# Rank terms on four row tiles of the array, from copies loaded four times over, in a low-rank modulated linear kernel

## The chip, the cores and the metric

The kernel runs on one core of a Trainium2 chip. The metric is device time in microseconds (us) for one launch, the median of three runs. The profile shows one execution; its engines are PE (the matrix engine, with its weight loads on the row PEld), DVE, ACT, POOL and SP.

## The reference, cut to what matters

Eight batches `b` of 1024 rows `t` and 512 features are sent through two layers with a residual sum each. The first layer's matrix belongs to the batch: a shared base plus a term of rank 8, whose factors come out of a small network on the condition vector. The second layer scales a shared weight by the condition on both sides.

```python
ae = layernorm(cond); h = gelu(ae @ w1 + b1); xw = h @ w2 + b2
x_a, x_b = split(xw)                        # each (b, 512, 8)
layer = base + einsum('bdr,bkr->bdk', x_a, x_b)
x = x + (x + einsum('btc,bco->bto', x, layer))
ys = cond / sqrt(512); d = rsqrt(einsum('bi,io->bo', ys*ys, weight*weight) + 1e-8)
x = x + einsum('bsi,io->bso', x * ys[:, None], weight) * d[:, None]
```

## The kernel before

The two layers and both residual sums are folded into one 512 x 512 matrix per batch, P(b) = (2I + base + A(b) B(b)^T) N(b), where N(b) = I + diag(ys) weight diag(d). P(b) is built in the tile `q[b]` as (2I + base) N(b) plus the rank term A(b) T(b), with T(b) = B(b)^T N(b), a product of small inner dimension. Then out = x P(b).

Matrices are held as a rounded part and a rest (`ph`, `pl` of `q`; the two halves of `xs` for x; `nh`, `nl` of N), and a product is three matmuls: high by high, high by low, low by high.

**The factors.** `stack` makes, for each group g of four batches, a tile `sa[g]` with A and a tile `stt[g]` with T. Their 128 partitions are four blocks of 32, one per batch: in a block lie the 8 ranks with their splits into high and low parts, so that one matmul over the 32 rows gives the rank term to full precision. Since the four batches share a tile, `mask_t` (line 487) multiplies `stt[g]` by a 0/1 column and so keeps one batch's 32 rows; `rank_term` (line 492) then contracts over all 128 rows, for one block `c` of 128 output rows.

**Setup** (lines 81 to 786) runs in an order written out by hand: weight loads, the small network (`px` gathers h @ w2; its matmuls run on column tiles of 32), the factors, the bases of batches 0 to 3 in units of six matmuls (`Fill`), and batch 0 whole. Here the buffers of PSUM are `misc` (2), `px` (2) and `acc` (4).

**Main stage** (lines 788 to 862). `main(b, t)` is 12 matmuls into one of four `po` buffers, a copy on ACT and a store. It runs 64 times; place i = 8b + t is the slot after the i-th of them. Everything else of batches 1 to 7 is put behind a place with `at(...)`:

- Batches 1 to 3: `rank_p` (line 634), one column block behind each of the places first+1 to first+4 with first = 0, 8, 16. It takes a `po` buffer, runs one matmul and adds the result to `q[b]` on DVE. `split_p` follows, which rounds half of `q[b]` into `ph` on ACT and subtracts into `pl` on DVE.
- Batches 4 and 5, and 6 and 7, are built in pairs by seven products in two halves each (`Pair`, 14 units of six matmuls, first = 14 and 29), which use the four `acc` buffers. Half of the rank terms are matmuls added into a product's own buffer (products 3 and 4, lines 598 and 599); the other half come from `ranks_11` and `ranks_22` at first+12 and first+13, in `po` buffers.

PE instructions are pinned in program order. In the main stage a scheduler orders DVE, ACT, POOL and SP instructions ahead of time; each engine then runs its queue strictly in order and waits on semaphores. A buffer of a pool is given out again when its last reader is done: `acc` has four, used in turn.

Of the kernel before, what the change touches and what calls it, by code (L numbers as in the profile page):

```python
# [7 lines left out]
F32 = mybir.dt.float32  # L8
F32R = mybir.dt.float32r
# [5 lines left out]
P = 128  # L15
NB = 8
NT = 1024
D = 512
KC = D // P
# [11 lines left out]
def cond_resid_kernel(ctx: ExitStack, tc: tile.TileContext, small, cond, condrows, consts,  # L31
# [10 lines left out]
    nc = tc.nc  # L42

    def mm(*args, **kw):
        tc.keep_in_program_order(nc.tensor.matmul(*args, **kw))  # L45
# [18 lines left out]
    ve, se, sy = InOrder(nc.vector), InOrder(nc.scalar), InOrder(nc.sync)  # L64

    cp = ctx.enter_context(tc.tile_pool(name="cp", bufs=1))
    npool = ctx.enter_context(tc.tile_pool(name="npool", bufs=2))
    ppool = ctx.enter_context(tc.tile_pool(name="ppool", bufs=2))
    big = ctx.enter_context(tc.tile_pool(name="big", bufs=9))
    dram = ctx.enter_context(tc.tile_pool(name="dram", bufs=1, space=bass.MemoryType.DRAM))  # L70
    acc = ctx.enter_context(tc.tile_pool(name="acc", bufs=4, space=PSUM))
    setup = ctx.enter_context(ExitStack())
    misc = setup.enter_context(tc.tile_pool(name="misc", bufs=2, space=PSUM))
    xps = setup.enter_context(tc.tile_pool(name="xps", bufs=1, space=PSUM))
    sp = setup.enter_context(tc.tile_pool(name="sp", bufs=1))

    def big_tile(name, dtype=F32):
        return big.tile([P, KC, D], dtype, tag="big", name=name)
# [20 lines left out]
    mask = cst[:, 2 * P + 5 + NB:2 * P + 5 + NB + 4]  # L99
# [61 lines left out]
    def newton_rsqrt(v, sd, shape, name):  # L161

        r = sp.tile(shape, F32, name=f"r_{name}")
        ve.reciprocal(r, sd)
        t = sp.tile(shape, F32, name=f"t_{name}")
        ve.tensor_mul(t, r, r)
        ve.tensor_mul(t, t, v)
        ve.tensor_scalar(t, t, -0.5, 1.5, ALU.mult, ALU.add)
        return r, t
# [12 lines left out]
    r, t = newton_rsqrt(ve_l, sd, [NB, 1], "l")  # L182
# [30 lines left out]
    q = {0: big_tile("q_0")}  # L213
# [71 lines left out]
    r, t = newton_rsqrt(v, sv, [P, KC, NB], "d")  # L285
# [19 lines left out]
    def work_tile():  # L305
        turns[0] += 1
        return work[:, turns[0] % KC, :]
# [99 lines left out]
    def split(src):  # L407
# [3 lines left out]
        ve.scalar_tensor_tensor(s, hi.bitcast(F32), neg_u, src, ALU.mult, ALU.add)  # L411
        return s

    def stack(srcs, neg, name, g):

        ps = misc.tile([P, D], F32, tag="misc", name=f"ps_{name}{g}")
        for i, src in enumerate(srcs):
            mm(ps, sel[:, g, :], src, start=(i == 0), stop=(i == len(srcs) - 1))
        hi = work_tile()
        se.copy(hi, ps)  # L420

        def rest():
            s = cp.tile([P, D], F32R, name=f"st_{name}{g}")
            ve.scalar_tensor_tensor(s, hi.bitcast(F32), neg, ps, ALU.mult, ALU.add)
            return s

        return rest
# [47 lines left out]
    def add_base(b):  # L475
        for c in range(KC):
            ve.tensor_add(q[b][:, c, :], q[b][:, c, :], b_nat[0][:, c, :])
# [6 lines left out]

    tm = {}

    def mask_t(b):
        g, i = divmod(b, 4)
        tm[b] = npool.tile([P, D], F32R, tag="tm", name=f"tm_{b}", bufs=2)
        ve.tensor_scalar_mul(tm[b], stt[g].bitcast(F32), mask[:, i:i + 1])  # L490

    def rank_term(ps, b, c, first):
        mm(ps, sa[b // 4][:, c * P:(c + 1) * P], tm[b], start=first, stop=True,
           skip_group_check=not first)

    class Base:

# [19 lines left out]
                self.at += 1  # L517

    class Pair:

# [60 lines left out]
        def unit(self):  # L584
            p, s = self.todo.pop(0)
            b, w, z = self.b, ("w", s), ("z", s)
            key = w if p in (1, 6, 7, 4) else z
            first = p in (1, 5, 2)
            if first:
                self.bank[key] = acc.tile([P, D], F32, tag="acc", name=f"pp_{b}_{p}_{s}")  # L590
            if (p, s) in ((1, 0), (6, 0)):
                i = b + (p == 6)
                q[i] = big_tile(f"q_{i}")
            bank = self.bank[key]
            self.product(p, s, bank, first)
            c11, c21 = q[b][:, s, :], q[b][:, 2 + s, :]
            c12, c22 = (q[b + 1][:, s, :], q[b + 1][:, 2 + s, :]) if b + 1 in q else (None, None)
            if p in (3, 4):
                rank_term(bank, b + (p == 3), s + 2 * (p == 4), False)
            if p == 1:  # L600
                se.copy(c11, bank)
            elif p == 5:
                se.copy(c21, bank)
            elif p == 6:
                se.copy(c12, bank)
            elif p == 3:
                ve.tensor_add(c12, bank, c12)
            elif p == 7:
                se.copy(c22, bank)
                ve.tensor_add(c22, c22, c21)  # L610
            elif p == 2:
                ve.tensor_add(c11, bank, c11)
            else:
                se.copy(c21, bank)
# [7 lines left out]
    def p_tiles(b):  # L622
        ph[b] = ppool.tile([P, KC, D], F32R, tag="ph", name=f"ph_{b}")
        pl[b] = ppool.tile([P, KC, D], F32R, tag="pl", name=f"pl_{b}")

    def split_p(b, j, part=None):

        at = slice(2 * j, 2 * j + 2)
        if part != 1:
            se.copy(ph[b][:, at, :], q[b][:, at, :])  # L630
        if part != 0:
            ve.tensor_sub(pl[b][:, at, :], q[b][:, at, :], ph[b][:, at, :].bitcast(F32))

    def rank_p(pool, tag, b, c):

        ps = pool.tile([P, D], F32, tag=tag, name=f"pr_{b}_{c}")
        rank_term(ps, b, c, True)
        ve.tensor_add(q[b][:, c, :], ps, q[b][:, c, :])

    xs = {}  # L640

# [2 lines left out]
    def load_x(b, h):  # L644
        raw[b, h] = big_tile(f"x_{b}_{h}")
        sy.dma_start(raw[b, h], x[b, h])

    def split_x(b, j, part=None):

        t = raw[b, j // 2][:, :, (j % 2) * 2 * P:(j % 2 + 1) * 2 * P]  # L650
        if part != 1:
            xs[b, j] = big.tile([P, 2, KC, 2 * P], F32R, tag="big", name=f"xs_{b}_{j}")
            se.copy(xs[b, j][:, 0], t)
        if part != 0:
            ve.tensor_sub(xs[b, j][:, 1], t, xs[b, j][:, 0].bitcast(F32))


    stt, sa = [None, None], [None, None]
# [86 lines left out]
    next(steps)  # L745
    w2_group()
    next(steps)
    mask_t(0)
    add_base(0)
    fill.units(2)  # L750
    fill.make_n(3, 0)
# [13 lines left out]
    fill.units(3)  # L765
    fill.make_n(3, 1)
    p_tiles(0)
    rank_p(misc, "misc", 0, 0)
    rank_p(misc, "misc", 0, 1)
    fill.round(3, 1)  # L770
    fill.units(2)
    split_p(0, 0, 0)
    rank_p(misc, "misc", 0, 2)
    rank_p(misc, "misc", 0, 3)
    split_p(0, 0, 1)
    fill.finish(3, 1)
    split_p(0, 1)
# [11 lines left out]
    po = ctx.enter_context(tc.tile_pool(name="po", bufs=4, space=PSUM))  # L789
# [18 lines left out]
    def at(b, t, f, *args):  # L808
        after.setdefault((b, t), []).append((f, args))
# [1 line left out]
    def new_pair(b):  # L811
        pairs[b] = Pair(b)

    def ranks_22(b):
        for i in range(2):
            rank_p(po, "po", b + 1, 2 + i)

    def ranks_11(b):
        for i in range(2):
            rank_p(po, "po", b, i)  # L820

    pairs = {}
    place = lambda i: divmod(i, NTT)
    for b in range(1, 4):
        first = (b - 1) * NTT
        for c in range(KC):
            at(*place(first + 1 + c), rank_p, po, "po", b, c)
            if c % 2:
                at(*place(first + 1 + c), split_p, b, c // 2)
    for b, first in ((4, 14), (6, 29)):  # L830

        at(*place(first - 9), load_d, b)
        at(*place(first - 6), new_pair, b)
        for n, p in enumerate(Pair.ORDER):
            at(*place(first - 5 + 2 * n), lambda b=b, p=p: pairs[b].early(p))
            at(*place(first - 2 + 2 * n), lambda b=b, p=p: pairs[b].prepare(p))
            for i in range(2):
                at(*place(first + 2 * n + i), lambda b=b: pairs[b].unit())
        at(*place(first + 5), mask_t, b + 1)
        at(*place(first + 7), mask_t, b)  # L840
        at(*place(first + 12), ranks_11, b)
        at(*place(first + 13), ranks_22, b)
        at(*place(first + 13), split_p, b, 0)
        at(*place(first + 14), split_p, b, 1)
        at(*place(first + 19), split_p, b + 1, 0)
        at(*place(first + 21), split_p, b + 1, 1)

    for b in range(NB):
        for t in range(NTT):
            last = b == NB - 1 and t == NTT - 1  # L850
            if t == 0 and b + 1 < NB:
                p_tiles(b + 1)
                if b < 3:
                    mask_t(b + 1)
            main(b, t, ((0, D // 2), (D // 2, D)) if last else ((0, D),))
            i = b * NTT + t
            if t % 4 == 0 and i + 4 < NB * NTT:
                load_x(*divmod(i // 4 + 1, NHALF))
            if t % 2 == 0 and i + 4 < NB * NTT:
                split_x(*divmod(i // 2 + 2, NTT // 2))  # L860
            for f, args in after.get((b, t), ()):
                f(*args)
# [69 lines left out]
```

## Time and profile before

| | |
|---|---|
| median of three runs | 305.82 us (305.3 to 306.11) |
| the profiled execution | 305.47 us, of which span 303.7 us |
| PE busy | 298.0 us, 98% |
| PEld busy | 227.9 us, 75% |
| DVE busy | 176.4 us, 58% |
| ACT busy | 145.9 us, 48% |
| POOL busy | 5.2 us, 2% |
| granted PE clock, mean | 0.998 |

1.8 us of the profiled execution lie around its span. Busy time of PE counts a matmul to its end, and matmuls overlap one another: of those with 512 columns each lasts about 0.39 us and the next starts 0.23 us after it. What a matmul costs a full queue is thus the distance of starts, which the timeline view gives, and not its duration.

### The profile page before, as it was taken

How to read it: one execution, taken by the hardware profiler on the slowest of the kernel's cores; microseconds unless marked ns; L12 is line 12 of the kernel's file. 1: busy time of each engine (PE TensorE's matmuls, PEld its weight loads, DVE VectorE, ACT ScalarE, POOL GpSimd, SP SyncE). 2: the span in 40 equal slices, each digit the busy share in tenths (PEclk: the TensorE clock that was granted, in tenths of full speed). 3: DMA queues.
4: the chain of work that ended last, by engine and by line, in shares of the span. 5: the costliest groups of instructions: out<-in, count | busy, mean ns of one | idle time of the engine just before them, and what ended most of it. 6: DMA issues, size and time to landing. Idle time of an engine off the chain costs nothing.

```text
span 303.7 us, 3551 instructions
## 1 busy us (share of the span) xinstructions
PE 298.0 (98%) x1369; PEld 227.9 (75%) x1369; DVE 176.4 (58%) x262; ACT 145.9 (48%) x212; POOL 5.2 (2%) x14
## 2 busy tenths in 40 slices
PE   8999999999999999999999999999999999999995
PEld 3655565466888888888888888888888888888884
DVE  4779830979678479977456478981266543600000
ACT  4756132256476564355664454743645546621221
POOL 0011000001000000100000000000000000000000
PEclk9999999999999999999999999999999999999999
DMA  6999999642319636631651134354151545322222
GB/s 204 409 427 419 410 421 419 220 188 69 138 69 343 242 124 226 228 120 69 207 193 52 69 108 171 97 162 192 69 207 69 190 178 212 148 106 104 96 76 105
DMA packets 15952, 57.37 MB, mean 189 GB/s; under 512 B 1840, under 2 KB 2352, under 8 KB 11584
## 3 DMA queue, kind: packets, MB, share of 16 engines
q1 hardware_dynamic: 6064, 38.78, 34.5%
q10 hardware_dynamic: 9360, 16.78, 14.7%
q0 software_dynamic: 512, 1.59, 1.6%
q8 instruction: 10, 0.16, 0.2%
q14 instruction: 6, 0.05, 0.1%
HBM read 40.35 MB, written 16.79 MB: 188 GB/s over the span
## 4 chain that ended last, share of the span: by engine, by line
PE 88%; DVE 5%; DMA 4%; ACT 2%; issue 0%; ACTq 0%
PE po L45 57%; PE pp L45 13%; PE pq L45 7%; DMA w<-in_w 4%; PE px L45 3%; PE warm L45 2%; PE pg L45 2%; DVE n L62 2%; PE pr L45 2%; PE pt_t L45 1%; ACT work L62 1%; DVE scr L62 0%; PE ps_t L45 0%; DVE q L62 0%; PE pq_v L45 0%
## 5 line engine op out<-in xcount | busy, mean ns | idle before, releaser
L45 PE MATMUL po<-ph,xs 128*128 128x512 f32 (+1 forms) x520 | 164.2, 386 | 0.0
L45 PEld LDWEIGHTS po<-ph,xs 128*128 128x128 f32 x520 | 97.1, 188 | 19.8
L45 PE MATMUL po<-pl,xs 128*128 128x512 f32 (+1 forms) x260 | 100.3, 386 | 0.0
L62 ACT COPY o<-po 128x512 f32<-128x512 f32 (+1 forms) x65 | 37.8, 581 | 87.0 <-PE po L45 86.8
L45 PEld LDWEIGHTS po<-pl,xs 128*128 128x128 f32 x260 | 48.8, 188 | 9.9
L62 DVE TENSOR_TENSOR xs<-x,xs 128x1024 fp32r<-128x1024 f32 x32 | 38.7, 1221 | 20.5 <-ACT xs L62 20.5
L62 ACT CAST xs<-x 128x1024 fp32r<-128x1024 f32 x32 | 33.0, 1050 | 4.0 <-DMA x<-in_x 2.3
L62 DVE TENSOR_TENSOR nl_p<-n,nh_p 128x1024 fp32r<-128x1024 f32 x14 | 17.1, 1220 | 20.0 <-ACT nh_p L62 20.0
L62 DVE TENSOR_TENSOR pl<-q,ph 128x1024 fp32r<-128x1024 f32 x16 | 19.4, 1220 | 7.3 <-ACT ph L62 7.3
L62 DVE TENSOR_TENSOR q<-pr,q 128x512 f32<-128x512 f32 x24 | 15.8, 685 | 7.9 <-PE pr L45 7.8
L45 PE MATMUL pq<-nh,bh 128*128 128x512 f32 x48 | 19.8, 412 | 0.0
L45 PE MATMUL pq<-nl,bh 128*128 128x512 f32 x48 | 19.1, 398 | 0.1
L45 PE MATMUL pq<-nh,bl 128*128 128x512 f32 x48 | 19.0, 395 | 0.0
L62 ACT CAST ph<-q 128x1024 fp32r<-128x1024 f32 x16 | 16.6, 1051 | 3.9 <-DVE q L62 3.7
L62 DVE SCALAR_TENSOR_TENSOR n<-w_sb,ysT,d 128x512 f32<-128x512 f32 x24 | 17.8, 745 | 0.8 <-DMA d<-d_out 0.8
L62 ACT COPY q<-pp 128x512 f32<-128x512 f32 x20 | 11.7, 587 | 13.3 <-PE pp L45 13.3
L45 PE MATMUL px<-w,hT 128*32 128x512 f32 x128 | 16.0, 601 | 0.4 <-DMA w<-in_w 0.4
L62 ACT CAST nh_p<-n 128x1024 fp32r<-128x1024 f32 x14 | 14.7, 1052 | 2.5 <-PE pp L45 2.4
L45 PEld LDWEIGHTS pq<-nh,bh 128*128 128x128 f32 x48 | 9.0, 188 | 8.4 <-issue 5.0
L45 PE MATMUL pp<-nh_p,sh 128*128 128x512 f32 x32 | 12.4, 389 | 0.0
L45 PE MATMUL pp<-nl_p,sh 128*128 128x512 f32 x32 | 12.4, 389 | 0.0
L45 PE MATMUL pp<-nh_p,sl 128*128 128x512 f32 x32 | 12.4, 389 | 0.0
(135 smaller groups left out, 272.9 us busy)
## 6 DMA issues: line engine op xcount, KB each, us to landing
w<-in_w SPq DMA_DIRECT2D x16, 1024.0 KB, 11.1
x<-in_x SPq DMA_DIRECT2D x16, 1024.0 KB, 5.2
out<-o ACTq DMA_DIRECT2D x63, 256.0 KB, 2.0
d<-d_out POOLq DMA_DIRECT2D x6, 256.0 KB, 3.9
w_sb<-in_weight SPq DMA_DIRECT2D x2, 512.0 KB, 5.4
b_raw<-in_baseT SPq DMA_DIRECT2D x2, 512.0 KB, 6.2
w_sb<-in_w SPq DMA_DIRECT2D x1, 1024.0 KB, 9.6
b_nat<-in_base SPq DMA_DIRECT2D x1, 1024.0 KB, 9.5
```

The source lines that it names most:

```text
L45: tc.keep_in_program_order(nc.tensor.matmul(*args, **kw))
L62: return lambda *a, **kw: pin(f(*a, **kw)) if InOrder.on else f(*a, **kw)
```

## The change

For batches 1 to 7 the masks go, and so does the contraction over 128 rows of which 96 are zero. `stack` now also stores both tiles of a group to DRAM (`kept`). A new `load_rank(b)` loads the batch's 32 rows of A and of T into a tile each (`fa`, `ft`), four times over, once into each block of 32 partitions: eight loads of 64 KB, on POOL's queue. The new `rank_term(b)` runs four matmuls of 32 rows, column block c on the row tile at partitions 32c, each into an `acc` buffer of its own, and four additions to `q[b]` on DVE. Batch 0 keeps its mask and its four full matmuls (`rank_first`).

The rank terms also move: for batches 1 to 3 to the places 2, 7 and 12, all four blocks at once; for a pair to first+14 and first+15, out of the products and out of `po`. `split_p` of a pair's first batch goes two places later, to first+15 and first+16.

```diff
+            kept[name, g] = dram.tile([P, D], F32R, name=f"kept_{name}{g}")
+            nc.gpsimd.dma_start(kept[name, g], s)
...
+    def load_rank(b):
+        for name in ("a", "t"):
+            g, i = divmod(b, 4)
+            fold[name, b] = npool.tile([P, D], F32R, tag=f"f{name}", name=f"f{name}_{b}", bufs=2)
+            for c in range(KC):
+                nc.gpsimd.dma_start(fold[name, b][32 * c:32 * c + 32, :],
+                                    kept[name, g][32 * i:32 * i + 32, :])
+
+    def rank_term(b):
+        ps = [acc.tile([P, D], F32, tag="acc", name=f"pr_{b}_{c}") for c in range(KC)]
+        for c in range(KC):
+            at = slice(32 * c, 32 * c + 32)
+            mm(ps[c], fold["a", b][at, c * P:(c + 1) * P], fold["t", b][at, :],
+               start=True, stop=True)
+        for c in range(KC):
+            ve.tensor_add(q[b][:, c, :], ps[c], q[b][:, c, :])
...
-            if p in (3, 4):
-                rank_term(bank, b + (p == 3), s + 2 * (p == 4), False)
...
-        for c in range(KC):
-            at(*place(first + 1 + c), rank_p, po, "po", b, c)
-            if c % 2:
-                at(*place(first + 1 + c), split_p, b, c // 2)
+        at(*place(max(0, 5 * b - 9)), load_rank, b)
+        at(*place(5 * b - 3), rank_term, b)
+        for j in range(2):
+            at(*place(first + 3 + j), split_p, b, j)
...
-        at(*place(first + 5), mask_t, b + 1)
-        at(*place(first + 7), mask_t, b)
-        at(*place(first + 12), ranks_11, b)
-        at(*place(first + 13), ranks_22, b)
-        at(*place(first + 13), split_p, b, 0)
-        at(*place(first + 14), split_p, b, 1)
+        at(*place(first + 2), load_rank, b)
+        at(*place(first + 4), load_rank, b + 1)
+        at(*place(first + 14), rank_term, b)
+        at(*place(first + 15), rank_term, b + 1)
+        at(*place(first + 15), split_p, b, 0)
+        at(*place(first + 16), split_p, b, 1)
...
-                if b < 3:
-                    mask_t(b + 1)
```

More of the change, by code (lines that the diff above doesn't have):

```diff
@@ L412, in split @@
         return s
+    kept = {}
     def stack(srcs, neg, name, g):
@@ L422, in rest @@
         def rest():
-            s = cp.tile([P, D], F32R, name=f"st_{name}{g}")
+            s = sp.tile([P, D], F32R, name=f"st_{name}{g}")
             ve.scalar_tensor_tensor(s, hi.bitcast(F32), neg, ps, ALU.mult, ALU.add)
+            kept[name, g] = dram.tile([P, D], F32R, name=f"kept_{name}{g}")
+            nc.gpsimd.dma_start(kept[name, g], s)
             return s
@@ L485, in cond_resid_kernel, with mask_t, rank_first @@
     tm = {}
[L487 to L494, printed above, removed]
+    def mask_t():
+        tm[0] = sp.tile([P, D], F32R, name="tm_0")
+        ve.tensor_scalar_mul(tm[0], stt[0].bitcast(F32), mask[:, 0:1])
+    def rank_first(c):
+        ps = misc.tile([P, D], F32, tag="misc", name=f"pr_0_{c}")
+        mm(ps, sa[0][:, c * P:(c + 1) * P], tm[0], start=True, stop=True)
+        ve.tensor_add(q[0][:, c, :], ps, q[0][:, c, :])
+    fold = {}
+    def load_rank(b):
[13 more added lines that the diff above has]
+            ve.tensor_add(q[b][:, c, :], ps[c], q[b][:, c, :])
     class Base:
@@ L632, in split_p @@
             ve.tensor_sub(pl[b][:, at, :], q[b][:, at, :], ph[b][:, at, :].bitcast(F32))
[L634 to L638, printed above, removed]
     xs = {}
@@ L747, in cond_resid_kernel @@
     next(steps)
-    mask_t(0)
+    mask_t()
     add_base(0)
@@ L767, in cond_resid_kernel @@
     p_tiles(0)
-    rank_p(misc, "misc", 0, 0)
-    rank_p(misc, "misc", 0, 1)
+    rank_first(0)
+    rank_first(1)
     fill.round(3, 1)
@@ L772, in cond_resid_kernel @@
     split_p(0, 0, 0)
-    rank_p(misc, "misc", 0, 2)
-    rank_p(misc, "misc", 0, 3)
+    rank_first(2)
+    rank_first(3)
     split_p(0, 0, 1)
@@ L812, in new_pair @@
         pairs[b] = Pair(b)
[L814 to L820, printed above, removed]
     pairs = {}
```

## The prediction

> **What bounds the kernel now.** I read the page first, then waits and timelines stage by stage.
>
> ```profile
> PE 298.0 (98%) x1369; PEld 227.9 (75%) x1369; DVE 176.4 (58%) x262; ACT 145.9 (48%) x212; POOL 5.2 (2%) x14
> PE 88%; DVE 5%; DMA 4%; ACT 2%; issue 0%; ACTq 0%
> ```
>
> The chain that ended last is PE for 88%, and the rest of it lies in setup: in the main stage (from 80.8 us on) the waits view names not one wait of PE. PE is a full queue there. A matmul taken out is worth its slot, and a wait put in front of PE is lost in full.
>
> The slot, from PE's timeline around the last rank terms of the first pair (columns: start, duration, count):
>
> ```profile
> 179.93 0.40 PE L45 MATMUL pp<-nh_p,bl 128*128 128x512 f32 x1
> 180.16 0.39 PE L45 MATMUL pp<-tm,st_a 128*128 128x512 f32 x1
> 180.39 0.61 PE L45 MATMUL pr<-tm,st_a 128*128 128x512 f32 x2
> 180.84 0.39 PE L45 MATMUL po<-ph,xs 128*128 128x512 f32 x1
> ```
>
> From 180.16 to 180.84 three rank matmuls take 0.68 us: 0.227 each, like their neighbours. A `main` is 12 x 0.227 = 2.72 us, a unit of a pair 1.38.
>
> The trace has no row tiles, but `px` runs on column tiles of 32, and the switch there and back is in setup's PE timeline:
>
> ```profile
> 62.52 0.40 PE L45 MATMUL pq<-nh,bl 128*128 128x512 f32 x1
> 62.84 1.07 PE L45 MATMUL px<-w,hT 128*32 128x512 f32 x8
> 63.84 0.51 PE L45 MATMUL pq<-nh,bh 128*128 128x512 f32 x1
> 64.19 0.39 PE L45 MATMUL pq<-nl,bh 128*128 128x512 f32 x1
> 64.42 0.39 PE L45 MATMUL pq<-nh,bl 128*128 128x512 f32 x1
> ```
>
> Eight tile matmuls fit in 1.00 us (62.84 to 63.84), so tiles do run side by side: two passes of four, 0.41 to 0.43 us each (longer runs of `px` show that pitch; its data are plain 4-byte, not the rounded kind). The switch: 0.32 instead of 0.23 before the first tile, 1.00 where two passes are 0.84, then 0.35 instead of 0.23 before the second full matmul, and the first full one lasts 0.51 instead of 0.39, since its weights were not loaded ahead. From 62.52 to 64.19 are 1.67 us; without tiles they would be 0.46. So 1.21 us for two passes of 0.41: 0.39 us are the switch.
>
> Last, DVE's timeline where the first pair ends:
>
> ```profile
> 176.01 1.29 DVE L62 TENSOR_TENSOR q<-pr,q 128x512 f32<-128x512 f32 x2 [1.79 <-PE pr L45]
> 177.21 0.74 DVE L62 SCALAR_TENSOR_TENSOR n<-w_sb,ysT,d 128x512 f32<-128x512 f32 x1
> 177.99 0.29 DVE L62 TENSOR_TENSOR n<-n,sm 128x128 f32<-128x128 f32 x1
> 178.20 0.74 DVE L62 SCALAR_TENSOR_TENSOR n<-w_sb,ysT,d 128x512 f32<-128x512 f32 x1
> 178.86 1.22 DVE L62 TENSOR_TENSOR pl<-q,ph 128x1024 fp32r<-128x1024 f32 x1
> 180.00 0.28 DVE L62 TENSOR_TENSOR n<-n,sm 128x128 f32<-128x128 f32 x1
> 185.12 0.48 DVE L62 TENSOR_SCALAR tm<-st_t,cst 128x512 fp32r<-128x512 f32 x1
> ```
>
> The slots of DVE come from the starts: an addition of 128x512 0.60 (two in 1.20), an `n` product 0.66 before independent work, `pl` 1.14, the small `n` sum 0.20. An addition starts 0.04 us after its matmul ends (175.58 + 0.39 = 175.97, then 176.01).
>
> **The change part by part.**
>
> *Removed from PE.* 28 full rank matmuls: 12 of batches 1 to 3, 16 of the pairs. 28 x 0.227 = 6.36 us, all on the path.
>
> *Added to PE.* Seven groups of four row tiles. One group: a pass of rounded data, 0.23; the switch, 0.39; and the entry must load 128 columns of weights per tile where `px` loads 32. The first full matmul after tiles shows what an uncovered 128-column load adds, 0.11; the first `px` showed some 0.03. So 0.08 more: 0.70 us a group. Bounds: [...] 1.38 above if tiles follow one another (0.70 + 3 x 0.227).
>
> [...] the row above puts 0.39 us on a round trip. Every group here is alone among full matmuls and pays it. I take 0.70, nearest to the rows.
>
> *The new wait.* The seven groups take all four `acc` buffers each. For batches 1 to 3 nobody needs them soon (the first pair starts two places after batch 3's group). Batch 4's group, at place 28, needs the buffers of the last product, copied by ACT (0.59 us) one `main` earlier: covered by 2.72. Batch 5's, at place 29, needs batch 4's four additions. And directly behind it in PE's order stands the first unit of the second pair, whose `acc` buffer is that of batch 5's block 0: it waits for DVE's addition. In the changed kernel's DVE order this addition stands behind batch 4's four, an `n` product, half a `pl`, a small `n` sum and an `n` product. With T the slot of batch 4's group:
>
> - Tiles start at T+0.10 and end at 0.62 (0.51 long); additions at 0.66, 1.26, 1.86, 2.46; the last ends at 3.14 (0.68 long).
> - `n` at 3.06; `pl` at 3.72 (ACT's `ph` needs two additions, 1.94, and 1.06 of its own: 3.03, in time); small sum at 4.86; `n` at 5.06; the addition for batch 5 at 5.72, ending 6.41. PE goes on at 6.45, and loses 0.11 to the uncovered weights: 6.56.
> - PE itself: 0.70, `main` 2.72, at 3.42 (buffers free since 3.14) batch 5's group, 0.70. It is through at 4.12 and waits 2.3 us.
>
> So these two groups and their `main` take 6.56 us, 3.84 without the `main`. Behind the waiting unit stands all of PE's queue, and ACT behind it. The second pair has the same two groups at places 43 and 44 but no unit behind them: no wait beyond the additions, which end 0.3 us ahead of need.
>
> *DVE.* Eight more additions (8 x 0.60), seven masks fewer (0.40 each by starts): 2.0 us more on an engine that is 58% busy. Elsewhere this is covered by PE's queue; at place 29 it is the wait above. `split_p` of batch 4 two places later: the last `pl` half ends about T+9.6, while `main` of batch 4 starts after three more units and two `main`, past T+15. Covered.
>
> *POOL and DMA.* Four stores of 256 KB and 56 loads of 64 KB; at 0.53 us an issue (row `d`, two in 1.06 to 1.10) some 32 us on an idle POOL. The rows land 3.9 us after issue. Batch 1 is the tightest: `st_a` is written at 68.6, a store may take 5.7 (row `d_out`), four issues 2.1 and 3.9 to land: 80.4, against a group after three `main`, 80.8 + 8.2 = 89.0. From batch 3 on a load waits for the group two batches before, 10 to 21 places ahead of need. The `d` loads of the second pair stand behind batch 5's, which wait for place 12; they had waited for later DVE work anyway. The first output copy on ACT now waits for the last store (about 84.0, when it is due at 83.9); `po` has four buffers, so PE would notice at 91.7. One place is tight: the first store is issued near 58 us, while the last w2 load is still coming, and PE takes that load up at 62.84 without a wait. 256 KB at the 420 GB/s of the full slices of setup are 0.6 us, of which I put 0.1 on the path (0 to 0.4).
>
> *Sum.* Five lone groups 5 x 0.70 = 3.50; the two at the pair 3.84; stores 0.1; less 6.36: +1.1 us. On the profiled execution 305.5 + 1.1 = 306.6; the median of the runs stands 0.35 above it, so 306.9.
>
> **The rivals.**
>
> *Cheap switch (ends faster).* [...] Against: two rows, each with 0.1 us lost on both sides. The break-even is 5G = 2.5, a group of 0.50; faster by 0.3% needs about 0.33.
>
> *Tiles in a row (slower).* The four do not overlap, because each needs its own 128-column load or the buffers hold the later ones back. Then 5 x 1.38 = 6.9; the pair stays near 3.84, DVE sets it: +4.4 us, 310.2. This is also the case in which the change doesn't do what it says. Against: the eight `px` in 1.00 us. In between, two and two, +2.2, 308.0.
>
> *Clock (slower).* PE idle for 2.3 us lets the clock fall. At the end of the trace it fell to 0.50 after some 2.3 to 2.6 us without matmuls (mean 0.94 over 300.2 to 302.8, 0.50 after). [...] By the row it can just happen[...]. It decides from a gap of about 2.3 on.
>
> **How the numbers follow.** A measurement of this kernel tells about 0.3% (0.9 us) from no change. The main case, chance 0.68: a group between 0.55 and 0.85 and the wait off by 0.3 give 305.9 to 307.9; 306.7 is the edge of 0.3%, so 0.40 slower and 0.28 the same. Tiles in a row or half so: 0.13, slower. Clock: 0.10, slower. Cheap switch: 0.09, of which 0.07 faster and 0.02 the same. Together faster 0.07, same 0.30, slower 0.63. The range takes in the clock and two-and-two, and part of the cheap switch: 305.0 to 309.0.
>
> **What would show it.** In the profile after: seven groups `pr<-ft,fa` of four starts within some 0.02 us, 0.70 us from slot to slot; one wait of PE (or its weight load) on DVE `q` of about 2.3 us, near 185 us, in front of the first `pp` of the second pair, and no other in the main stage; no wait on `fa` or `ft`; a clock of 1.0 throughout; the last `px` of setup at 62.8 to 63.2. I am wrong if starts in a group are 0.2 us apart, if a group costs under 0.5, if that wait is missing, or if loads hold a group back.

## The result and the profile after

The changed kernel is slower: 307.49 us median of 11 executions (305.92 to 309.17), against 305.3 (304.95 to 306.73) beside it, a ratio of 1.006 with a 95% interval from 1.0037 to 1.0084. The executions of the changed kernel fall apart by the granted clock: three with a mean clock of 1.00 took 305.92, 306.19 and 306.33 us, eight with 0.994 or less took 307.47 to 309.17. The profile below is of the one that took 306.19, so it shows the change without the fall of the clock.

From the page (busy time of the engines, shares of the chain), and from the view of the tile `po` (first and last start of the main stage's matmuls, after the duration's minimum, median and maximum in ns; the last row is that of the kernel before):

```profile
PE 296.5 (97%) x1369; PEld 223.4 (73%) x1369; DVE 177.6 (58%) x263; ACT 145.5 (48%) x212; POOL 34.7 (11%) x74
PE 87%; DVE 7%; DMA 4%; ACT 2%; issue 0%; ACTq 0%
L45 PE MATMUL po<-ph,xs x520: 278/389/504, 80.8 to 300.8; 128*128 128x512 f32 x168, 128*128 128x256 f32 x6
L45 PE MATMUL po<-ph,xs x520: 277/389/396, 80.8 to 299.9; 128*128 128x512 f32 x168, 128*128 128x256 f32 x6
```

PE is 1.5 us less busy, and DVE's share of the chain rises from 5 to 7%: PE now waits for it. The main stage starts at 80.8 as before and its last matmul at 300.8 where it was 299.9: 0.9 us lost there, none in setup.

The waits of the main stage, all of PE's (total, times, longest):

```profile
PEld pp L45 <- DVE q L62: 2.8, 1, 2.8
PE pp L45 <- DVE q L62: 2.4, 1, 2.4
PEld pr L45 <- issue: 1.8, 5, 0.4
PEld po L45 <- issue: 1.5, 6, 0.2
PEld pr L45 <- DVE q L62: 0.7, 2, 0.4
```

Before there was none. The two "issue" rows are on weight loads, at the entries into groups and behind them, where the distances below show what the switch costs. The first two rows are one wait, once, in front of a `pp`. PE's timeline shows where:

```profile
180.84 0.39 PE L45 MATMUL po<-ph,xs 128*128 128x512 f32 x1
181.16 0.51 PE L45 MATMUL pr<-ft,fa 32*128 32x512 f32 x4
181.60 0.50 PE L45 MATMUL po<-ph,xs 128*128 128x512 f32 x1
181.94 0.39 PE L45 MATMUL po<-pl,xs 128*128 128x512 f32 x1
...
184.23 0.39 PE L45 MATMUL po<-ph,xs 128*128 128x512 f32 x1
184.55 0.50 PE L45 MATMUL pr<-ft,fa 32*128 32x512 f32 x4
187.50 0.51 PE L45 MATMUL pp<-nh_p,bh 128*128 128x512 f32 x1 [2.44 <-DVE q L62]
187.84 0.39 PE L45 MATMUL pp<-nl_p,bh 128*128 128x512 f32 x1
```

Four tile matmuls fit in 0.51 us together, so they run side by side: 0.49 each, and 0.01 from the first start to the last. Around them the distances are 0.32, 0.44 and 0.34 instead of 0.23. Batch 5's group at 184.55 is through by 185.05; the next matmul of PE starts at 187.50. What DVE did meanwhile:

```profile
181.70 2.48 DVE L62 TENSOR_TENSOR q<-pr,q 128x512 f32<-128x512 f32 x4 [0.36 <-PE pr L45]
184.10 0.74 DVE L62 SCALAR_TENSOR_TENSOR n<-w_sb,ysT,d 128x512 f32<-128x512 f32 x1
184.76 1.22 DVE L62 TENSOR_TENSOR pl<-q,ph 128x1024 fp32r<-128x1024 f32 x1
185.89 0.29 DVE L62 TENSOR_TENSOR n<-n,sm 128x128 f32<-128x128 f32 x1
186.09 0.75 DVE L62 SCALAR_TENSOR_TENSOR n<-w_sb,ysT,d 128x512 f32<-128x512 f32 x1
186.75 0.69 DVE L62 TENSOR_TENSOR q<-pr,q 128x512 f32<-128x512 f32 x1
```

DVE is never idle from 181.70 to the addition at 186.75 that frees the buffer, 1.70 us after the tiles of its group are through: behind the four additions of batch 4 come two `n` products, a small sum and half a `pl`. Experiment 3 takes three of these four rows out of the way.

### The profile page after: what moved, and what is told of

The parts are those of the page before. It is cut to its first block, busy times and chain, and to the rows that moved or that the text cites. A ratio compares the mean times of both kernels' runs of the same rounds, so it can differ in the third digit from the quotient of the medians.

```text
span 304.4 us, 3654 instructions
## 1 busy us (share of the span) xinstructions
PE 296.5 (97%) x1369; PEld 223.4 (73%) x1369; DVE 177.6 (58%) x263; ACT 145.5 (48%) x212; POOL 34.7 (11%) x74
## 4 chain that ended last, share of the span: by engine, by line
PE 87%; DVE 7%; DMA 4%; ACT 2%; issue 0%; ACTq 0%
PE po L45 57%; PE pp L45 13%; PE pq L45 7%; DMA w<-in_w 4%; PE px L45 3%; DVE n L62 2%; PE warm L45 2%; PE pg L45 2%; DVE q L62 1%; PE pr L45 1%; PE pt_t L45 1%; ACT work L62 1%; DVE scr L62 0%; PE ps_t L45 0%; DVE pl L62 0%
## 5 line engine op out<-in xcount | busy, mean ns | idle before, releaser
L509 POOL DMA_DIRECT2D fa<-kept_a x28 | 13.7, 507 | 86.7 <-PE pr L45 86.6
L62 DVE TENSOR_TENSOR q<-pr,q 128x512 f32<-128x512 f32 x32 | 20.1, 685 | 3.8 <-PE pr L45 3.8
L509 POOL DMA_DIRECT2D ft<-kept_t x28 | 13.8, 515 | 4.9 <-DMA kept_t<-st_t 4.9
```

The source lines that it names most:

```text
L62: return lambda *a, **kw: pin(f(*a, **kw)) if InOrder.on else f(*a, **kw)
L509: nc.gpsimd.dma_start(fold[name, b][32 * c:32 * c + 32, :], kept[name, g][32 * i:32 * i + 32, :])
```

## The experiments

**1. What does a group cost, and what of it is the switch?** The groups of batches 1 to 3 run their four tiles twice:

```diff
             mm(ps[c], fold["a", b][at, c * P:(c + 1) * P], fold["t", b][at, :], start=True, stop=True)
+        for c in range(KC if b < 4 else 0):
+            at = slice(32 * c, 32 * c + 32)
+            mm(ps[c], fold["a", b][at, c * P:(c + 1) * P], fold["t", b][at, :], start=True, stop=True)
```

> The changed kernel with the four row-tile matmuls of batches 1, 2 and 3 issued twice in a row into the same buffers (the second pass overwrites the first with the same values). It measures what a group costs by itself and what the switch costs. Theory (0.64 us a group is 0.23 us of tile work and 0.41 us of switching there and back): a second pass starts 0.21 to 0.24 us behind the first, and three of them add 0.7 us to the span, 305.1 with the clock at 1.00. Rival (a group costs 0.6 us because its tiles load 128 columns of weights each, one after the other, or stream more slowly): 0.4 to 0.64 us from pass to pass, 1.2 to 1.9 us more.

PE's timeline at the group of batch 1, with the weight loads of its tiles, and below it the two rows of the changed kernel:

```profile
89.08 0.74 PE L45 MATMUL pr<-ft,fa 32*128 32x512 f32 x8
89.08 0.30 PEld L45 LDWEIGHTS pr<-ft,fa 32*128 32x128 f32 x8 [0.35 <-issue]
89.75 0.50 PE L45 MATMUL po<-ph,xs 128*128 128x512 f32 x1
89.06 0.50 PE L45 MATMUL pr<-ft,fa 32*128 32x512 f32 x4
89.49 0.50 PE L45 MATMUL po<-ph,xs 128*128 128x512 f32 x1
```

From the first tile to the next full matmul are 0.67 us, where the single pass of the changed kernel takes 0.43. The second pass thus costs 0.24 us. Its first tile starts at 89.41, 0.33 behind the first pass and not 0.21 to 0.24 as expected: the weights of the group are loaded only from 89.08 on, with the first tile and not ahead of it (eight loads, 0.30 us, to 89.38). The exit is shorter by as much. Tile work (0.24 us) is a third of a group (0.66 to 0.69, see experiment 4), and the rest is the switch.

The single execution took 308.81 us, with a span of 307.0, 2.6 above the changed kernel's profile, where three passes account for 0.7. It was one in which the clock fell, the only one of these with a trace, and it shows what that is. Its row of the clock on the page, the windows view (length, then busy time and count of PE, PEld, DVE, ACT, POOL, then the granted clock, DMA share and GB/s), and PE's timeline:

```profile
PEclk9999999999999999999999997999999999999999
185.13:188.54 3.41, 0.96 (x7) 0.58 (x7) 3.41 (x7) 1.23 (x2) 3.41 (x8) 1.00 0.68 185
188.54:191.95 3.41, 3.41 (x10) 2.63 (x9) 2.64 (x4) 1.22 (x2) 1.90 (x4) 0.50 0.60 153
191.95:195.36 3.41, 3.41 (x17) 2.75 (x16) 3.07 (x4) 0.90 (x2) 0.00 (x0) 1.00 0.00 0
185.16 0.50 PE L45 MATMUL pr<-ft,fa 32*128 32x512 f32 x4
188.11 0.50 PE L45 MATMUL pp<-nh_p,bh 128*128 128x512 f32 x1 [2.45 <-DVE q L62]
188.45 0.54 PE L45 MATMUL pp<-nl_p,bh 128*128 128x512 f32 x1
188.79 0.63 PE L45 MATMUL pp<-nh_p,bl 128*128 128x512 f32 x1
189.21 0.63 PE L45 MATMUL pp<-nh_p,bh 128*128 128x512 f32 x1
```

The same wait of 2.45 us stands there; right behind it the clock is 0.50 for 3.41 us, and matmuls start 0.43 us apart instead of 0.23. From 188.45 to 192.09 there are nine distances, 3.64 us where 9 x 0.227 = 2.04 would do: 1.6 us. Between the two sorts of executions of the changed kernel lie 1.3 (307.5 less 306.2). Of the 2.6 us some 0.3 stay open.

**2. Is it the idle array that brings the clock down?** Eight full matmuls that nobody reads fill the wait:

```diff
         at(*place(first + 15), rank_term, b + 1)
+        if b == 4:
+            at(*place(first + 15), keep_busy, 8)   # 8 x mm(ps, bh[:, 0, 0:P], bh[:, 0, :]), ps from po
```

> The changed kernel with eight full matmuls (batch-independent data, into a spare po buffer that nobody reads) put behind batch 5's group, inside the wait of 2.4 us; they take 8 x 0.227 = 1.8 us of it, and nothing waits for them. Theory (the wait costs twice: once as 2.4 us, and in most executions once more [...]): the clock is 1.00 in every execution, the span 304.1 to 304.6 in all of them, the median near 306.1, 1.4 below the changed kernel's 307.5, about 1.003 of the kernel before. Rival (the spread of the changed kernel comes from its 56 loads on POOL's queue or from the DMA, not from the idle array): the median stays near 307.5, 1.006, with the clock at 0.994 in most executions.

```profile
184.52 0.50 PE L45 MATMUL pr<-ft,fa 32*128 32x512 f32 x4
184.95 2.08 PE L45 MATMUL busy<-bh 128*128 128x512 f32 x8
187.47 0.50 PE L45 MATMUL pp<-nh_p,bh 128*128 128x512 f32 x1 [0.43 <-DVE q L62]
```

The unit starts at 187.47, where it started at 187.50: the fill costs nothing and leaves 0.43 us of idling. The clock was 0.994 in one of 14 executions, against 0.994 or less in eight of 11 (and in the one of experiment 1, which ran on the same chip as these 14). Why it fell in that one is not shown. The median is 306.31 us, a ratio of 1.0046 (1.0024 to 1.0067), not the 1.003 expected: three executions took 307.68 to 308.44 with the clock up, and what held them is not shown. So the count of clocks is clear; the gain in time (1.2 us by the medians) is less so, since the intervals of the two ratios overlap.

**3. Is DVE's order what makes the wait long?** The `n` products of the second pair's product 5 are made two places later:

```diff
-            at(*place(first - 5 + 2 * n), lambda b=b, p=p: pairs[b].early(p))
+            at(*place(first - 5 + 2 * n + 2 * (b == 6 and p == 5)), lambda b=b, p=p: pairs[b].early(p))
```

> The changed kernel with the n products of the second pair's product 5 made two places later, so that they and half a pl no longer stand in front of batch 5's first addition in DVE's queue. Theory (the length of the wait is set by what stands ahead of that addition in DVE's order): the addition starts right behind its group, the wait shrinks from 2.4 to 0.8-1.0 us, the clock stays at 1.00, and the time is 303.4 + 0.9 = 304.3, ratio 0.997. Rival (the wait hangs on something else, such as the weights or the first unit's right-hand side): it stays at 2.4 us, 306 to 307.5.

DVE's timeline and PE's:

```profile
181.78 2.48 DVE L62 TENSOR_TENSOR q<-pr,q 128x512 f32<-128x512 f32 x4 [0.36 <-PE pr L45]
184.19 1.23 DVE L62 TENSOR_TENSOR pl<-q,ph 128x1024 fp32r<-128x1024 f32 x1
185.33 2.48 DVE L62 TENSOR_TENSOR q<-pr,q 128x512 f32<-128x512 f32 x4
184.66 0.51 PE L45 MATMUL pr<-ft,fa 32*128 32x512 f32 x4
186.07 0.50 PE L45 MATMUL pp<-nh_p,bh 128*128 128x512 f32 x1 [0.89 <-DVE q L62]
```

Three of the four rows in between are gone (an `n` product, the sum and the other `n` product), the addition starts 0.16 us after its tiles end (184.66 + 0.51), and the wait is 0.89 us. No execution of 14 had a clock under 0.997. 304.83 us, ratio 0.9988 (0.9978 to 0.9998). DVE's order set the length of the wait; without a buffer shared there would still be some.

**4. Without the wait.** The second pair starts one place later, so that a `main` lies between:

```diff
-    for b, first in ((4, 14), (6, 29)):
+    for b, first in ((4, 14), (6, 30)):
```

> The changed kernel with the whole second pair one place later (first = 30 for 29), so that one main of 2.72 us lies between batch 5's group and the first unit that takes its buffer. Theory (the one wait of 2.4 us, and the clock after it, is all that the change loses): no wait of PE in the main stage, clock 1.00; seven groups at 0.64 instead of 28 slots of 0.227: 4.5 - 6.4 = -1.9 us, 303.4 against 305.3 before, ratio 0.994. Rival (the wait is DVE's backlog, and moves to batch 6, whose splits now end one place later): a new wait of PE in front of batch 6's first main, over 0.5 us, and 304.5 or more.

All of PE's waits in its main stage, and its row of `po`:

```profile
PEld pr L45 <- issue: 1.8, 5, 0.4
PEld po L45 <- issue: 1.7, 7, 0.2
PEld pr L45 <- DVE q L62: 0.7, 2, 0.4
L45 PE MATMUL po<-ph,xs x520: 277/389/504, 80.6 to 298.1; 128*128 128x512 f32 x168, 128*128 128x256 f32 x6
```

304.26 us, ratio 0.9967 (0.9955 to 0.9979). No wait of PE for DVE is left except 0.7 us on weight loads at batch 5's and 7's groups, whose entries are no longer than those of the other groups (0.32 us), and none came up at batch 6. The clock stayed up. The gain is 1.0 us, though, where 1.9 was expected. On PE's main stage it is 1.6 (217.5 us for 219.1): the 0.64 us a group that the expectation used was read from the first three distances at the switch, and the following matmuls are a little late as well. Counted over the `main` behind it, a group costs 0.66 to 0.69 us, so seven cost up to 4.8. The rest of the difference lies outside: from the start of the last matmul to the end of the span are 4.1 us for 3.8 before, and 2.1 us of an execution lie around its span for 1.8. Why is open.

**5. Tiles or places?** Two versions with the tiles undone (masks and full matmuls, at the new places, in `acc`), one with the pair where the change has it and one with the pair later; and the version of experiment 4 again beside them:

```diff
-                nc.gpsimd.dma_start(fold[name, b][32 * c:32 * c + 32, :], kept[name, g][32 * i:32 * i + 32, :])
+        ve.tensor_scalar_mul(tm[b], stt[g].bitcast(F32), mask[:, i:i + 1])
...
-            mm(ps[c], fold["a", b][at, c * P:(c + 1) * P], fold["t", b][at, :], start=True, stop=True)
+            mm(ps[c], sa[b // 4][:, c * P:(c + 1) * P], tm[b], start=True, stop=True)
```

Full matmuls, the pair not moved:

> The changed kernel with the tiles undone and its places and buffers kept: masks on DVE instead of stores and loads, and each group four full matmuls of 128 rows (batch 5's group still directly in front of the unit that takes its buffer). Theory (the wait comes from the places and from acc, not from the tiles): PE comes to the unit 0.4 to 0.7 us later, so the wait is 1.6 to 1.8 us and nothing else changes against the kernel before: 305.2 + 1.7 = 306.9, ratio 1.0055, clock 1.00 if a gap of 1.7 us is too short for it to fall. Rival (the wait belongs to the tiles or to their loads): no wait, 305.2.

The wait is there without any tile or load, in PE's timeline:

```profile
185.74 1.07 PE L45 MATMUL pr<-tm,st_a 128*128 128x512 f32 x4
188.34 0.50 PE L45 MATMUL pp<-nh_p,bh 128*128 128x512 f32 x1 [1.53 <-DVE q L62]
```

It is 1.53 us, the clock never fell, and the main stage takes 220.9 us (81.2 to 302.1), 1.8 more than before, 1.5 of it the wait. The median of four executions is 308.11 us, ratio 1.0078 (1.0051 to 1.0106), over a microsecond above the expectation. Of that, 0.4 us are the kernel before, which took 305.58 beside it where the expectation reckoned with 305.2, and 0.4 lie in setup by its profile (first `po` at 81.2 for 80.8), where the first `px` is late by as much already (20.1 for 19.7), ahead of all that the edit touches; the rest is open.

Full matmuls, the pair later:

> The tiles undone as in the run before, and the second pair one place later, so that there is no wait: beside the changed kernel with the pair later, only the tiles with their stores and loads differ. Theory (a tile group costs 0.69 us of PE with all that follows the switch, four full matmuls 0.91): as long as the kernel before, 305.2, ratio 1.000, PE's main stage 219.1 us. Rival (what the later pair won came from the placing, not from the tiles): 304.3, ratio 0.997, like the version with tiles.

And the tiles with the pair later, again:

> The changed kernel with the second pair one place later once more, on the same chip as the version with the tiles undone. Theory: 304.2, ratio 0.997, and 1.0 us (1.5 on PE) below the version with full matmuls. Rival: no difference between the two.

305.68 us, ratio 0.9996 (0.9981 to 1.0011), for full matmuls; 304.39 us, ratio 0.996 (0.9948 to 0.9972), for tiles. The view of the tile `po`, full matmuls first, tiles second:

```profile
L45 PE MATMUL po<-ph,xs x520: 278/390/397, 80.5 to 299.6; 128*128 128x512 f32 x168, 128*128 128x256 f32 x6
L45 PE MATMUL po<-ph,xs x520: 278/390/505, 80.4 to 297.9; 128*128 128x512 f32 x168, 128*128 128x256 f32 x6
```

Main stages of 219.1 us, like the kernel before, and 217.5. Placing the pair later wins nothing by itself; the tiles win 1.6 us on PE, as 28 x 0.227 - 7 x 0.69 = 1.5 has it. This last version beats both kernels: 0.4% faster than the one before, 1% than the changed one. Of the 1.6 us some 1.3 show in the medians; in the two profiled executions, 305.43 and 304.16, the spans differ by 1.7 (303.7 and 302.0), and the time around the span takes 0.4 of it back, which stays open.

## Why the prediction was right, and where not

*A group of tiles, put at 0.70 us.* Measured 0.66 to 0.69. The row of `px` at its switch was the right neighbour: a pass inside tile mode costs 0.24, and the switch comes on top.

*The one new wait, put at 2.3 us near 185 us in front of the second pair's first `pp`.* Measured 2.44, from 185.05 to 187.50. The order of DVE's rows came true row by row: with T at 181.07, the addition was put at T+5.72 (186.79) and started at 186.75. That it was the only wait in front of a matmul, and that batches 4 and 6 and all loads were covered, came true too.

*Stores and loads, put at 0.1 us (0 to 0.4).* Nothing: the last `px` of setup starts at 62.82 (62.84 before), the main stage at 80.8. POOL's 56 loads took 0.5 us each to issue, as estimated.

*The sum, +1.1 us.* For executions with the clock up it is right: 0.7 us between the two profiled executions, 0.9 on PE's main stage.

*The clock, a rival with a chance of 0.10.* This is the step that failed: the sum leaves it out, and it belonged in. Its place was right, and it costs 1.6 us in the trace of experiment 1 and 1.3 between the executions; but it came in eight of 11 executions, and so it decides the median: 307.5 and not 306.2. The prediction had a row for it, the end of the trace, where the clock fell after 2.3 to 2.6 us without matmuls. The chance of 0.10 was the author's estimate. The runs decide for the row: a gap of 2.44 us was enough more often than not; with one of 1.53 (four executions) or 0.89 (14) it did not happen. The last section has the rows.

*The rival of tiles in a row* is refuted by the four that fit in 0.51 us. *The rival of a cheap switch*, an estimate of the author, is too: it needed a group under 0.50 us. The forecast of slower with 0.63 thus holds, for the wait that it named and a second loss behind it that it had rated too low. The measured time, 307.49, lies within 305.0 to 309.0. There is luck in how clearly the forecast holds. With the clock up, the three executions at 306.2 stand 0.9 us above the 305.3 of the kernel before, just on the 0.3% that the prediction set as the edge between slower and the same; the rest came from a rival with a chance of 0.10. The number, too, came closer than the change: 307.5 for 306.9 looks near, but the 306.9 was 1.1 us on top of 305.8, and the kernel before took 305.3 beside the changed one, so the loss was 2.2 us where 1.1 was put.

## What to carry to other kernels

Cost a switch into tile mode as an entry and an exit around the group, from a place in the trace where the array already switches, and not by the speedup of the tile work: a lone group of four (0.66 to 0.69 us) saves a quarter of what four full matmuls cost (0.91), where its tile work alone (0.24) would save three quarters. When work moves to a pool of buffers that the next work on the full engine takes from, follow the queue of the engine that frees them, row by row. And count an idle stretch of PE of the length seen here, 2.4 us, twice: as itself, and as a stretch at half clock that may follow (3.41 us in one trace).

## What was not expected of the hardware

The granted clock can fall after an idle stretch of 2.4 us, and not in every execution of the same program: eight of 11 with 2.44 us, one of 14 with the stretch filled to 0.43, none of 14 with 0.89 and none of four with 1.53. After the fall the array ran at a clock of 0.50 for 3.41 us (experiment 1, the one trace of such a fall) and lost 1.3 to 1.6 us.

The length of the idle stretch alone does not tell whether the clock falls. The wait of 2.44 us in the changed kernel's profile passed at a clock of 1.00, and right behind the one of 2.45 us in experiment 1 it was 0.50. The ends of the traces differ as well. The windows view shows the last matmuls and what follows them, first for the tiles with the pair later (experiment 4), then for full matmuls with the pair later (experiment 5):

```profile
296.93:300.35 3.42, 1.48 (x13) 1.28 (x11) 0.00 (x0) 0.75 (x2) 0.00 (x0) 1.00 0.43 153
300.35:302.16 1.81, 0.00 (x0) 0.00 (x0) 0.00 (x0) 0.00 (x0) 0.00 (x0) 0.50 0.02 5
298.26:301.67 3.41, 1.67 (x14) 1.46 (x13) 0.00 (x0) 0.74 (x2) 0.00 (x0) 1.00 0.43 154
301.67:303.65 1.98, 0.00 (x0) 0.00 (x0) 0.00 (x0) 0.00 (x0) 0.00 (x0) 1.00 0.01 5
```

In the first the last matmul ends at 298.41 (296.93 + 1.48), and from 300.35 on, 1.94 us later, the clock is 0.50. In the second it ends at 299.93 (298.26 + 1.67), and the clock is still 1.00 when the span ends at 303.65, 3.7 us later. In the profile of the kernel before it is 0.50 from 302.5 on, 2.3 us after the last matmul (300.21); in the changed kernel's it is 1.00 up to the end at 304.4, 3.3 us after the last (301.07). What decides is not shown, and neither is it that each of the eight executions fell behind the wait, since none of them has a trace.
